# Cross-attention on one core: the value products of two head quads in one run of TensorE, in every second slot

## The chip, the cores and the metric

The kernel runs on one core of one Trainium2 chip. The metric is the time on the device in microseconds (us); a kernel is run several times, and the median counts. Everything is in float32. TensorE (PE) multiplies, VectorE (DVE), ScalarE (ACT) and GpSimd (POOL) work on tiles in SBUF and PSUM, and all DMAs but two small ones are issued by SyncE (SP), whose queue is worked off in order.

## The reference

A layer of cross-attention over 8 batches of 256 rows and 256 memory slots, with 1024 columns in 32 heads of 32. It is cut here to what is computed:

```python
mu = jnp.mean(hidden_states, axis=-1, keepdims=True)
var = jnp.var(hidden_states, axis=-1, keepdims=True)
x = (hidden_states - mu) * jax.lax.rsqrt(var + LN_EPS) * ln_gamma + ln_beta
Q = _split_heads(x @ Wq.T)
K = _split_heads(memory_keys)
V = _split_heads(memory_values)
scores = jnp.einsum('bhsd,bhtd->bhst', Q, K) * scale
scores = jnp.where(mask, scores, -jnp.inf)
probs = jax.nn.softmax(scores, axis=-1)
attn = jnp.einsum('bhst,bhtd->bhsd', probs, V)
attn = attn.transpose(0, 2, 1, 3).reshape(B, S, HIDDEN)
return residual + attn @ Wout.T
```

Keys and values are both the input `ctx_4096`. The mask is all ones, but the kernel works for any.

## The kernel before, in words

The unit of work is a *quad*: four heads of one batch, which fill the 128 partitions. There are 8 quads in a batch and N = 64 in all. The main loop (L903) has one *slot* per quad n; `b, i = divmod(n - 8, 8)` gives the batch whose output is projected meanwhile, and the place i of the slot in that batch. A kernel is written here in the order in which each engine is to do its work (a manual schedule), and waits follow from the data.

In slot n TensorE is given, in this order:

- `scores(n + 1)` (L471): 8 matmuls on four tiles of 32 rows, into four PSUM banks;
- the output steps of place 0 (`project_steps(n, 0)`);
- `values(n - 2)` (L614), the *value run*: 32 matmuls, probabilities times values, on eight tiles of 64 rows by 32 columns. A float32 matmul is two records of PE and two weight loads, so the run has 64 and 64. It fills two PSUM tiles, and ACT copies them with `copy_at` (L629) into `at`, the operand of the output projection;
- the output steps of place 1, then the query projection (`make_q` L331 in the first slots, later `query_product` L432), then the output steps of place 2.

The output projection of a batch is done by seven products of half-size blocks (a Strassen scheme, `PRODUCTS` L647), each in four steps of 128 rows, so 28 steps a batch. `STEPS` (L654) deals them to nine slots, i = 0 to 8, and in each slot to the three places. Step 0 to 3 are A11, 4 to 7 A12, 8 to 11 S2, then S3, A22, S1 and S4. Step c of A12 reads quad 4 + c of the batch. Blocks and sums are taken or stored between steps by DVE (`take`, `store`), since all go through one PSUM bank. The sums S1 to S4 are made by POOL (`sum_at`). Batch 6 is dealt by `ENDS` to slots 56 to 63, and the last batch is projected in part in slots 59 to 62 and in part behind the loop (L1013 to L1078).

The softmax of quad n + 1 (`softmax_parts`, L491) runs beside slot n on the other engines: DVE takes scores out of PSUM with the mask and the row minimum, ACT takes the exponential, POOL divides, and DVE transposes blocks of 32 into `pT`. A quarter of `pT` stands on wrong partitions; ACT copies it aside into `pc` (`aside`), and four DMAs of SP, the *swaps*, put it in its place (`tail`, L595). Loads named in `ahead` go out before the swaps, those in `between` stand between the first two swaps and the last two. In slots below 8 and above 56 the tail is put off into the next softmax (L604). `copy_at` stands in that stream of ACT behind the first exponentials, or, in slots with i = 1, behind the last.

`load_v` (L140) brings the values of a pair of quads, 512 KB, in odd slots for the next pair, into one of two buffers (`vp`). `pT` has three buffers, `pc` (`asp`) three.

## Time and profile before

| what | us |
|---|---|
| median of 3 runs | 575.77 |
| lowest, highest run | 574.71, 577.12 |
| profiled execution, span | 577.6 |
| PE busy | 567.7 |
| DVE busy | 458.6 |
| ACT busy | 412.1 |
| POOL busy | 404.7 |
| value products on PE (L622), 4096 records | 74.3 |

The profile gives no other time for its execution than the span, from the first instruction to the last. It is 1.8 us above the median and 0.5 above the highest of the runs. PE's granted clock is 0.997 on average.

A line of the timeline has the start, the length, the engine, the line of the kernel, the operation, what is written and read, the shape and the number of records, and in brackets the idle time of the engine before it with what ended it. A line of the waits has who waited for whom, the total in us, the number of times and the longest. A line of the stretches has the stretch, its length, then the busy time of PE, PE's weight loads, DVE, ACT and POOL with the instructions of each, then the granted clock, the share of the DMA engines and GB/s.

### The profile page before, as it was taken

What the parts mean: (1) busy time and instruction counts of PE and PEld (TensorE: products, weight loads), DVE (VectorE), ACT (ScalarE), POOL (GpSimd) and SP (SyncE); (2) the same over time, 40 slices, a digit from 0 to 9 for tenths busy, and PEclk for the clock granted to TensorE, in tenths of its full rate; (3) what the DMA queues carried; (4) which work ended last, traced back from release to release, by engine and by line L of the source; (5) the groups of instructions that cost most, each with busy time, mean ns of one, the idle gap of its engine ahead of it and who ended that gap; (6) DMA issues with size and microseconds to landing.
All of it is one profiled execution on the core that took longest, in us unless ns stands there. A gap on an engine that the chain in (4) does not pass through costs nothing.

```text
span 577.6 us, 20001 instructions
## 1 busy us (share of the span) xinstructions
PE 567.7 (98%) x7162; PEld 392.2 (68%) x7162; DVE 458.6 (79%) x1695; ACT 412.1 (71%) x1425; POOL 404.7 (70%) x672
## 2 busy tenths in 40 slices
PE   8999998999999999899999999999999999999998
PEld 8788884666667777477776677667766777755444
DVE  6897887687878878678888888888877868879823
ACT  4688886677758857678577976779767866869820
POOL 1788998699896896665657775676656667448780
PEclk9999999999999999999999999999999999999999
DMA  8675778756778667776686767887658865436741
GB/s 312 224 211 184 218 240 209 244 172 196 196 229 271 215 188 219 225 222 202 181 247 181 233 196 201 237 257 217 186 160 254 239 192 147 130 112 182 214 154 74
DMA packets 47475, 117.98 MB, mean 204 GB/s; under 512 B 9104, under 2 KB 9872, under 8 KB 47376
## 3 DMA queue, kind: packets, MB, share of 16 engines
q1 hardware_dynamic: 47088, 116.69, 68.2%
q8 instruction: 57, 0.93, 0.7%
q14 instruction: 42, 0.34, 0.2%
q10 hardware_dynamic: 288, 0.01, 0.0%
HBM read 65.28 MB, written 11.53 MB: 133 GB/s over the span
## 4 chain that ended last, share of the span: by engine, by line
PE 79%; POOL 8%; DVE 6%; issue 2%; DMA 2%; ACT 1%; SPq 0%; DVEq 0%; POOLq 0%; ACTq 0%
PE po_S L694 17%; PE pq_A L440 16%; PE sc L479 10%; PE po_A L694 10%; PE pv L622 9%; PE pq_S L440 6%; POOL e L528 6%; PE pq L340 6%; DVE e L515 3%; PE po_end L761 2%; DVE pT L534 1%; PE po_last L761 1%; POOL wo L183 1%; DMA pT<-pT 1%; ACT e L519 1%
## 5 line engine op out<-in xcount | busy, mean ns | idle before, releaser
L528 POOL TENSOR_SCALAR e<-e,rden 128x256 f32<-128x256 f32 x512 | 237.0, 483 | 131.1 <-DVE rden L526 129.6
L519 ACT ACTIVATE e<-e,mn 128x256 f32<-128x256 f32 x512 | 254.0, 500 | 53.8 <-DVE mn L515 53.8
L534 DVE STREAM_TRANSPOSE pT<-e 128x512 f32<-128x512 f32 x256 | 180.7, 707 | 54.8 <-POOL e L528 43.8
L515 DVE CUSTOM_DVE_ANT_0 e<-sc,mb 128x256 f32<-128x256 f32 x512 | 185.9, 416 | 23.7 <-PE sc L479 23.2
L540 ACT COPY pc<-pT 128x512 f32<-128x512 f32 x128 | 79.0, 617 | 72.0 <-DVE pT L534 43.0
L519 ACT ACTIVATION_READ_ACCUMULATOR e<-e,mn 128x1 f32 x512 | 97.7, 191 | 0.0
L340 PE MATMUL pq<-xnT,wq 128*128 128x256 f32 (+1 forms) x368 | 84.1, 383 | 0.0
L340 PEld LDWEIGHTS pq<-xnT,wq 128*128 128x128 f32 x368 | 68.7, 190 | 14.3 <-issue 3.9
L479 PEld LDWEIGHTS sc<-k,qa 32*128 32x128 f32 x1024 | 46.2, 184 | 42.4 <-issue 20.6
L694 PE MATMUL po_S<-wo,at 128*128 128x512 f32 x152 | 74.5, 607 | 0.3 <-DVE r L736 0.3
L622 PE MATMUL pv<-pT,v 64*32 64x128 f32 x4096 | 74.3, 274 | 0.0
L622 PEld LDWEIGHTS pv<-pT,v 64*32 64x32 f32 x4096 | 56.9, 105 | 25.3 <-issue 11.9
L479 PE MATMUL sc<-k,qa 32*128 32x256 f32 x1024 | 73.6, 400 | 0.1
L694 PE MATMUL po_A<-wo,at 128*128 128x512 f32 x128 | 61.9, 616 | 4.2 <-issue 2.2
L694 PE MATMUL po_S<-wo,s 128*128 128x512 f32 x104 | 50.2, 606 | 0.3 <-DVE r L736 0.3
L515 DVE DVE_READ_ACCUMULATOR2_ANT mn<- 128x1 f32 x512 | 42.6, 83 | 0.0
L694 PEld LDWEIGHTS po_A<-wo,at 128*128 128x128 f32 x128 | 22.6, 190 | 29.2 <-issue 23.4
L526 DVE RECIPROCAL rden<-den 128x2 f32<-128x2 f32 x256 | 37.5, 146 | 5.9 <-ACT e L519 4.6
L440 PEld LDWEIGHTS pq_A<-xnT,wq 128*128 128x128 f32 x320 | 37.3, 192 | 4.8 <-issue 4.1
L694 PEld LDWEIGHTS po_S<-wo,at 128*128 128x128 f32 x152 | 25.6, 190 | 20.8 <-issue 19.3
L440 PE MATMUL pq_A<-xnT,wq 128*128 128x128 f32 x320 | 37.3, 275 | 0.0
L635 ACT COPY at<-pv 128x128 f32<-128x128 f32 x128 | 26.2, 253 | 8.7 <-PE pv L622 8.7
(95 smaller groups left out, 605.3 us busy)
## 6 DMA issues: line engine op xcount, KB each, us to landing
v<-in_kv_dram SPq DMA_DIRECT2D x32, 512.0 KB, 4.2
pT<-pT SPq DMA_DIRECT2D x128, 128.0 KB, 2.9
pT<-pc SPq DMA_DIRECT2D x128, 128.0 KB, 4.7
ring<-kept_T SPq DMA_DIRECT2D x18, 512.0 KB, 5.8
k<-in_kv_dram SPq DMA_DIRECT2D x32, 256.0 KB, 3.0
x<-in_x_dram SPq DMA_DIRECT2D x14, 512.0 KB, 5.5
r<-in_x_dram SPq DMA_DIRECT2D x28, 256.0 KB, 4.5
out_dram<-r SPq DMA_DIRECT2D x28, 256.0 KB, 3.9
```

The source lines that it names most:

```text
L340: nc.tensor.matmul(pqs[n], wq[:, o, c, :], xnTs[b](c), start=(c == 0), stop=(c == NC - 1),)
L440: nc.tensor.matmul(pqs[b][:, o, :], w[:, c], x_[:, c], start=begins and o + c == 0, stop=c == NK - 1, skip_group_check=True,)
L479: nc.tensor.matmul(scs[n][j][:, s, :], qa[r, n % NQ, ts(s, P)], ks[n - n % 2][r, n % 2, :], start=True, stop=True,)
L515: nc.vector.tensor_tensor_reduce(out=e[:, s, :], in0=pss[j][:, s, :], in1=mbs[n // NQ], scale=1.0, scalar=NO_SCORE, op0=ALU.add, op1=ALU.m ...
L519: nc.scalar.activation(e[:, s, :], e[:, s, :], AF.Exp, bias=mn[:, s : s + 1], scale=-1.0, accum_out=den[:, s : s + 1],)
L526: nc.vector.reciprocal(rden, dens[j])
L528: nc.gpsimd.tensor_scalar(es[j][:, s, :], es[j][:, s, :], rden[:, s : s + 1], 1.0, ALU.mult, ALU.mult,)
L534: nc.vector.transpose(pT[:, :, :, j, :, :].rearrange("p a i s k -> p (a i) s k"), es[j].rearrange("p s (b t) -> p b s t", t=K),)
L540: nc.scalar.copy(pc[:, :, ts(j, 2)], pT[:, 1, :, ts(j, 2)])
L622: nc.tensor.matmul(pvs[n][r][j * HD : (j + 1) * HD], vs[n - n % 2][ts(r, 2 * K), i, ds(n % 2 * P + j * HD, HD)], pT[ts(r, 2 * K), :, i, j, ...
L635: nc.scalar.copy(ats[b, k][:, c, :, ts(r, 2), :], pv.rearrange("p a s k -> p s a k"))
L694: nc.tensor.matmul(po, operand(b, name)[:, c], wo[:, which, c], start=begins and c == 0, stop=c == NK - 1, skip_group_check=not begins,)
```

## The change

`values` takes one or two quads. Odd slots from 3 on call it with quads n - 3 and n - 2, whose 64 matmuls then stand in one run; even slots have no value products. The two PSUM tiles hold both quads, and `copy_at` moves both in each of its two instructions. Quads 62 and 63 behind the loop stay single.

A quad of an even number is so used one slot later. `pT` gets a fourth buffer; to make room the values have one buffer and `pc` two. `load_v(n - 1)` goes out in odd slot n, ahead of the swaps of that slot's softmax, into the buffer that the value run of the slot has just read. The values of the last pair go into a spare half of an `x` tile, in slot 58.

The 28 output steps are dealt anew over the same nine slots: even slots get more and odd ones fewer. In batch 6 the sum S2 is split two and two instead of three and one, as quad 6 of the batch is now there a slot later.

```diff
-    vp = ctx.enter_context(tc.tile_pool(name="vp", bufs=2))
+    vp = ctx.enter_context(tc.tile_pool(name="vp", bufs=1))
...
-    ptp = ctx.enter_context(tc.tile_pool(name="ptp", bufs=3))
-    asp = ctx.enter_context(tc.tile_pool(name="asp", bufs=3))
+    ptp = ctx.enter_context(tc.tile_pool(name="ptp", bufs=4))
+    asp = ctx.enter_context(tc.tile_pool(name="asp", bufs=2))
...
-        vs[n] = vp.tile([P, NI, 2 * P], F32, tag="v", name=f"v_{n}")
+        if n == N - 2:
+            spare = xp.tile([P, NS, D], F32, tag="x", name=f"v_{n}")
+            vs[n] = spare[:, 0].rearrange("p (i v) -> p i v", i=NI)
+        else:
+            vs[n] = vp.tile([P, NI, 2 * P], F32, tag="v", name=f"v_{n}")
...
-    def values(n):
-        pvs[n] = [
-            ps_v.tile([P, 2, NS, K], F32, tag="pv", name=f"pv_{n}_{r}") for r in range(2)
+    def values(*quads):
+        pair = pvs[quads] = [
+            ps_v.tile([P, len(quads), 2, NS, K], F32, tag="pv", name=f"pv_{quads[0]}_{r}")
+            for r in range(2)
         ]
...
+        for at, n in enumerate(quads):
+            pT = pTs.pop(n)
+            for i in range(NI):
+                for j in range(NH):
+                    for r in range(2):
+                        nc.tensor.matmul(
+                            pair[r][j * HD : (j + 1) * HD, at],
+                            vs[n - n % 2][ts(r, 2 * K), i, ds(n % 2 * P + j * HD, HD)],
+                            pT[ts(r, 2 * K), :, i, j, :, :],
+                            start=(i == 0), stop=(i == NI - 1),
+                        )
...
-        for r, pv in enumerate(pvs.pop(n)):
+        for r, pv in enumerate(pvs.pop(quads)):
             nc.scalar.copy(
-                ats[b, k][:, c, :, ts(r, 2), :], pv.rearrange("p a s k -> p s a k")
-            )
+                ats[b, k][:, ds(c, len(quads)), :, ts(r, 2), :],
+                pv.rearrange("p c a s k -> p c s a k"),
+            )
...
-    STEPS = ((0, 0, 0), (4, 0, 3), (0, 1, 2), (0, 2, 2), (0, 2, 1), (0, 1, 2), (0, 0, 3), (0, 1, 2),
-             (0, 2, 0))
+    STEPS = ((0, 0, 0), (4, 0, 3), (0, 1, 3), (0, 1, 1), (0, 3, 1), (0, 2, 0), (0, 1, 3), (0, 1, 1),
+             (0, 3, 0))
...
-        if n % 2 and n + 1 < N:
-            between.append(partial(load_v, n + 1))
-        elif n % 2 == 0 and n + 4 < N:
+        if n % 2 == 0 and n + 4 < N:
             between.append(partial(load_k, n + 4))
-        ahead = rings[n]
+        ahead = list(rings[n])
...
+        if n % 2 and 3 <= n < N - 1:
+            ahead.insert(0, partial(load_v, n - 1))
+        elif n == N - NQ + 2:
+            ahead.append(partial(load_v, N - 2))
...
-        if n >= 2:
-            values(n - 2)
+        if n >= 3 and n % 2:
+            values(n - 3, n - 2)
...
-            copy_at(n - 2)
+            copy_at((n - 3, n - 2))
...
-            sum_at(b, "S2", *((slice(NK - 1, NK),) if b == B - 2 else ()))
+            sum_at(b, "S2", *((slice(2, NK),) if b == B - 2 else ()))
...
-                sum_at(b, "S2", slice(0, NK - 1))
+                sum_at(b, "S2", slice(0, 2))
```

More of the change, by code (lines that the diff above doesn't have):

```diff
@@ L612, in softmax_parts, with copy_at @@
         yield
-    def values(n):
-        pvs[n] = [
-            ps_v.tile([P, 2, NS, K], F32, tag="pv", name=f"pv_{n}_{r}") for r in range(2)
-        ]
-        pT = pTs.pop(n)
-        for i in range(NI):
-            for j in range(NH):
-                for r in range(2):
-                    nc.tensor.matmul(
-                        pvs[n][r][j * HD : (j + 1) * HD],
-                        vs[n - n % 2][ts(r, 2 * K), i, ds(n % 2 * P + j * HD, HD)],
-                        pT[ts(r, 2 * K), :, i, j, :, :],
-                        start=(i == 0), stop=(i == NI - 1),
-                    )
-    def copy_at(n):
-        b, c = divmod(n, NQ)
+    def values(*quads):
+        pair = pvs[quads] = [
+            ps_v.tile([P, len(quads), 2, NS, K], F32, tag="pv", name=f"pv_{quads[0]}_{r}")
+            for r in range(2)
+        ]
+        for at, n in enumerate(quads):
[9 more added lines that the diff above has]
+                        )
+    def copy_at(quads):
+        b, c = divmod(quads[0], NQ)
         k, c = divmod(c, NK)
@@ L1042, in xattn_kernel @@
     values(N - 2)
-    copy_at(N - 2)
+    copy_at((N - 2,))
     end_sum(slice(2, 3), nc.gpsimd)
@@ L1050, in xattn_kernel @@
     values(N - 1)
-    copy_at(N - 1)
+    copy_at((N - 1,))
     end_sum(slice(3, 4), nc.vector)
```

## The prediction

> **What bounds the kernel.** I read the page's busy shares first, then who TensorE waits for, then its timeline slot by slot, then granted clock by stretch, last the end of the chain.

> ```profile
> PE 567.7 (98%) x7162; PEld 392.2 (68%) x7162; DVE 458.6 (79%) x1695; ACT 412.1 (71%) x1425; POOL 404.7 (70%) x672
> ...
> q8 instruction: 57, 0.93, 0.7%
> ```

> PE is busy 98%; the next, DVE, 79%. What shortens PE's stream shortens the kernel, wherever nothing else is due just behind. The second line is the queue that fetches instructions: 57 packets.

> ```profile
> PE po_A L694 <- issue: 2.2, 1, 2.2
> PE po_A L694 <- DMA wo<-in_woT_dram: 1.7, 1, 1.7
> ...
> PE po_S L694 <- DVE r L736: 0.6, 2, 0.3
> PE po_end L761 <- ACT at L635: 0.4, 1, 0.4
> ```

> These are nearly all of PE's waits. Two early ones are gates: PE waits for `wo` until 98.06, and at 106.15 for DVE's store, whose residual tile landed at 105.22.

> ```profile
> 251.60 1.15 PE L479 MATMUL sc<-k,qa 32*128 32x256 f32 x16
> 252.68 1.16 PE L622 MATMUL pv<-pT,v 64*32 64x128 f32 x64
> 253.76 1.98 PE L694 MATMUL po_S<-wo,s 128*128 128x512 f32 x4
> ```

> One slot's beginning: scores, value products, output steps. From the start of the value run to the start of the next, 1.08 to 1.09 us. Instruction by instruction the run is eight rounds on eight tiles; rounds begin at 0, 133, 242, 351, 461, 570, 679 and 788 ns, and the next run at 1.086 us. A round in the middle takes 0.109 us.

> ```profile
> 240.41 1.16 PE L622 MATMUL pv<-pT,v 64*32 64x128 f32 x64
> 243.75 1.87 PE L694 MATMUL po_A<-wo,at 128*128 128x512 f32 x2 [2.19 <-issue]
> ...
> 244.00:246.00 2.00, 2.00 (x5) 0.97 (x5) 0.34 (x1) 0.65 (x4) 0.00 (x0) 0.50 0.88 258
> ```

> Right behind a value run PE stands for 2.19 us with nothing to wait for. In the trace an instruction packet begins at 241.28, takes 1.10 us, and PE goes on at 243.75: it had run out of instructions. The last line (timeline above, stretches below) has granted clock 0.50: after this idle the trace's clock record stays at half for 3.41 us, so the event cost 2.19 + 1.70 = 3.9 us. A 1.71 us idle before 98.06 left the clock at 1.00.

> ```profile
> 547.67 1.02 PE L761 MATMUL po_last<-wo,at 128*128 128x512 f32 x2
> 548.63 1.16 PE L622 MATMUL pv<-pT,v 64*32 64x128 f32 x64
> 549.71 1.98 PE L761 MATMUL po_end<-wo,at 128*128 128x512 f32 x4
> 552.05 1.98 PE L761 MATMUL po_end<-wo,at 128*128 128x512 f32 x4 [0.36 <-ACT at L635]
> 553.97 1.16 PE L622 MATMUL pv<-pT,v 64*32 64x128 f32 x64
> ```

> The last slot: values of quad 61, two output steps with chunk 0 (quad 60, copied long before) while ACT works through the last softmax, then chunk 1, 0.36 us after ACT's copy.

> **The change, part by part.**

> *Merged value runs.* 64 runs become 31 double and 2 single ones. A second quad in the same run should add eight rounds: 8 x 0.109 = 0.875 us against 1.086 in a run of its own, so 1.961 for two. No double run is in the trace. Bounds for the second quad: 0.788 (from the first round's beginning to the last's) and 1.086 (it saves nothing). I take 0.875, what the rounds show inside one run. The re-entry into full-array matmuls (1.91 us for four records behind a value run against 1.72 behind a query product) is paid in even slots too, behind scores; it is not saved.

> *Where it counts.* What is saved before 106 is lost at the two gates: the load of `wo` was issued at 85.89 behind 1.3 MB, whose sum is not altered by the new order, and the residual at 100.48 behind the same swaps. From 106.15 to the scores of quad 63 (541.98) PE did quads 9 to 59, 51 x 1.086 = 55.39; now pairs (8,9) to (58,59), 26 x 1.961 = 50.99. With 0.29 for the second wait for DVE (149.76; slot 15 now reaches it 0.85 later) the gain is 4.69 us. The new deal of 28 steps changes no count: a step is 0.86 us wherever it stands.

> *The end.* In slot 63 quads 60 and 61 are now one run, and ACT copies both only behind the last softmax. That chain hangs on the scores of 63 and reaches the copies 9.6 us after them (541.98 to 551.57), as before. PE has then done its double run by 549.5 (old clock) and has no chunk 0 to do: it stands until the copies end. Two copies of 256 columns: 253 ns at 128 columns and 617 at 512 give 0.37 each, so about 552.3 against 552.00. Then four steps, 1.91 + 1.72 = 3.63, and values of 62 at 555.93 instead of 553.97: a loss of 1.96. Its bounds: 1.7 (two steps moved behind the copies) and 3.0 (the load of v 60 now goes out behind the two 512 KB loads that landed at 544.26 and 546.90). And the stand of 2.8 us is longer than the 2.19 that cost the clock: 1.70 more, bounds 0 and 1.7; by the nearest row, 1.70. [...]

> *Instructions in time.* PE's 14,554 recorded instructions are 256 to a packet of 16,384 bytes. Anchored at the stall, every packet begins at most 298 instructions ahead of its need, and 0.9 to 6.2 us after PE passes that point (median 1.5; 1.0 to 1.4 where nothing is queued). From packet to resumed PE took 2.47. So PE must need at least 3.5 us for 297 instructions, and more where the queues are full. A value run holds 128 instructions in 1.09 us. Laying the instruction lists of both kernels in such windows, with the trace's durations: before, the shortest is 5.8 us, and it is the very one that stalled; the next is 7.4. After, a double run holds 256 in 1.96 us: behind slot 10 there are three windows of 4.4 to 4.5 (slots 27, 36/37, 39), five of 5.7 to 6.9 and six of 7.1 to 8. Twelve packets of odd slots that were called for as early in the slot came 0.9 to 4.0 late, on the mean 0.29 above the 2.0 that a 4.5 window leaves: 3 x 0.29 = 0.87. In slots with i = 1, with delays 5.8, 5.1, 3.7 and 1.6, the windows of 6.2 and 6.9 cost 0.9 and 0.5 on the mean. Sum 2.3 us, and one half-clock stretch, 1.7. Bounds: 0, and 11 (three stalls of 2.0 + 1.7). [...]

> *One buffer of values.* The load waits for the double run of its slot; behind it on SP's queue stand the swaps of the next quad and the residual loads. SP gets there only after the swaps of the softmax before, 6 to 9 us into the slot; the run ends 3.0 into it (6.7 where i = 1). The load, 4.2 us to landing, has until the next odd slot, 17 us: nothing; with that cover gone PE would wait out what is left of the 4.2. That swaps now queue behind 512 KB (2.2 us) falls on even quads, which are used a slot later.

> *Copies, buffers, steps.* ACT's copy waits for the double run (0.35 us later), with exponentials queued behind; scores find their banks read 3 to 5 us earlier in most slots. At i = 1 the third A12 step now needs quad 6 from this slot: copies done at 7.45, step due at 8.58 (slot from 302.65). With `pc` on two buffers, aside waits for the swap of two slots before, landed 7 us earlier. Each nothing; if the 1.1 us at i = 1 went, 6 slots would pay.

> **Sum.** 577.6 - 3.9 (the profile's own stall) - 4.69 + 1.96 + 1.70 + 2.3 + 1.7 = 576.7. The profiled execution lies 1.8 above the median 575.77 and 0.5 above the highest run; without its stall it would be 573.7, a microsecond under the lowest (574.71). The runs thus hold events of this kind too, and I add none for them. Forecast 576.5.

> **Rivals.**
> - *Fetches keep up, the clock holds:* 573.7 - 4.69 + 1.96 = 571.0, with the clock lost at the end 572.7. For it: 53 of 57 packets came within 5.2 us; against it: the only short window before is the one that stalled.
> - *Slower, by the fetch alone:* double runs outrun the packets. It decides where a packet begins over 2.0 us after its call in a 4.5 window, and each time then loses the clock; two such with 2.0 + 1.7 on top of 572.7 give 580.1, three 583.8. For it: 19 of 51 packets from 60 us on were over 2.0.
> - *The second quad saves nothing:* 26 x 2.172 instead of 50.99 loses the gain and 0.8: with the other terms 582.2; against it: the rounds' even pace. That the runs are not merged is excluded: the built list has 256 value instructions together.

> **How the numbers follow.** My own sum 0.44 (573 to 578.6), the first rival 0.23, the second 0.25, the third 0.08. Half a per cent, about what a measurement of this kernel can tell from no change, is 572.9 to 578.65. The first rival is faster, the second and third slower, mine the same. Eight in ten: 571.8 to 581.5.

> **What would show it.** Value runs of 1.96 us in odd slots only; even slots 8.3 us long; PE "issue" waits right behind double runs, with clock 0.50 after them; some 2.8 us of PE idle before the first po_end, ended by ACT's copy. Wrong it is if double runs take 2.1 or if "issue" stays at nothing.

## The result and the profile after

The changed kernel takes 599.05 us (median of 4 runs, 592.69 to 600.71), and the kernel before took 575.24 beside it: a ratio of 1.0393, 95% interval 1.0335 to 1.0450. The prediction was 576.5 with a range up to 581.5; it was 22.6 us too low, and the change makes the kernel slower.

The profiled execution of the changed kernel has a span of 596.4 us, 18.8 more than the profiled one before (the medians are 23.8 apart; the execution profiled before was a long one, with a stand that the prediction puts at 3.9 us). From its page, the busy times, the queue that fetches instructions, and the chain of work that ended last:

```profile
PE 571.1 (96%) x7162; PEld 398.9 (67%) x7162; DVE 458.1 (77%) x1695; ACT 410.3 (69%) x1363; POOL 403.7 (68%) x672
...
q8 instruction: 56, 0.92, 0.7%
...
PE 65%; DMA 8%; POOL 8%; DVE 8%; ACT 4%; issue 3%; SPq 3%; DVEq 0%; ACTq 0%; POOLq 0%
```

The same chain of the kernel before:

```profile
PE 79%; POOL 8%; DVE 6%; issue 2%; DMA 2%; ACT 1%; SPq 0%; DVEq 0%; POOLq 0%; ACTq 0%
```

DMA has gone from 2% to 8% of the chain, and SP's queue, which was not on it, has 3%. Whom PE waits for in the changed kernel (total, times, longest):

```profile
PE pq_S L444 <- DMA ring<-kept_T: 5.0, 4, 2.8
PE po_A L693 <- ACT qa L353: 4.3, 1, 4.3
PE pv L628 <- DMA pT<-pT: 3.7, 3, 1.5
PE po_end L760 <- ACT at L641: 1.8, 1, 1.8
PE pv L628 <- ACT e L523: 1.4, 1, 1.4
...
PE pv L628 <- issue: 0.5, 1, 0.5
```

Before, the list was led by one stand for instructions and one for `wo`. Now PE waits for the ring's weights, for query copies and for swaps, and hardly for instructions. The start of each slot (its first scores) against the same slot before tells where the 18.8 us come from:

| place | us against before |
|---|---|
| up to slot 9 | -1.0 |
| slot 9 | +5.5 |
| slots 10 to 30, without the kernel before's own stand in slot 26 | +2.5 |
| that stand and its half clock | -3.9 |
| slots 31 to 41 | +6.2 |
| slot 42 (a ring wait of 2.84 us, then half clock) | +5.9 |
| slots 43 to 61 | +1.8 |
| behind the scores of quad 63 | +1.8 |

An odd slot's beginning in the timeline of the changed kernel (start, length, engine, line, operation, shape, records):

```profile
255.82 1.15 PE L483 MATMUL sc<-k,qa 32*128 32x256 f32 x16
256.90 2.11 PE L628 MATMUL pv<-pT,v 64*32 64x128 f32 x128
258.93 1.13 PE L693 MATMUL po_S<-wo,s 128*128 128x512 f32 x2
```

A double run takes 2.03 us from its start to the next operation's (2.036 is usual), where two single ones took 2.17. So the runs are merged and mostly save 0.136 a pair, not 0.211. Three of the 31 do take 1.96 us, the prediction's figure, and 10 of 30 in the fastest kernel below; what sets the two apart is not shown.

Slot 9, PE first, then ACT, then the granted clock (0.50, ahead of the DMA share) in a stretch behind the wait:

```profile
87.13 1.15 PE L483 MATMUL sc<-k,qa 32*128 32x256 f32 x16
92.53 6.34 PE L693 MATMUL po_A<-wo,at 128*128 128x512 f32 x8 [4.26 <-ACT qa L353]
98.81 2.11 PE L628 MATMUL pv<-pT,v 64*32 64x128 f32 x128
```

```profile
91.48 0.62 ACT L544 COPY pc<-pT 128x512 f32<-128x512 f32 x1 [4.58 <-DMA pT<-pc]
92.01 0.83 ACT L353 ACTIVATE qa<-pq,qa 128x256 f32<-128x256 f32 x2
```

```profile
92.40:95.00 2.60, 2.47 (x3) 1.17 (x4) 1.51 (x10) 2.60 (x10) 2.60 (x3) 0.50 0.98 294
```

ACT wants to copy into one of two `pc` buffers that a swap of two quads before still reads; the query copy stands behind it, and PE's next steps need the bank that this copy empties. That swap was issued at 83.14, right behind a load of `wo`, and landed 7.9 us later. Eight records then take 6.34 us at half clock instead of 3.70.

SP's queue in the same stretch of work, the kernel before first:

```profile
226.71 1.14 SPq L600 DMA_DIRECT2D pT<-pT  x2
227.91 0.58 SPq L144 DMA_DIRECT2D v<-in_kv_dram  x1
228.53 0.44 SPq L407 DMA_DIRECT2D ring<-kept_T  x1
229.07 1.15 SPq L604 DMA_DIRECT2D pT<-pc  x2
```

The changed kernel:

```profile
236.22 0.40 SPq L148 DMA_DIRECT2D v<-in_kv_dram  x1
236.72 1.15 SPq L604 DMA_DIRECT2D pT<-pT  x2
237.92 0.57 SPq L411 DMA_DIRECT2D ring<-kept_T  x1
241.41 1.20 SPq L608 DMA_DIRECT2D pT<-pc  x2
```

The last two swaps write where the first two read, so SP holds them until the first two have landed. Before, SP filled that time with the load and stood 0.1 us. Now it stands from 238.49 to 241.41, 2.9 us in which it issues nothing else; the first two swaps land late, behind 512 KB (median to landing 4.2 us against 2.9). It is so throughout: at the 25 even quads from 8 to 56, whose swaps are the ones behind the load, SP stands 1.3 to 6.7 us for their landing, median 3.1 (before, 0.0). This ring load is 9.4 us later than before, though PE is only some 5 us behind. What that ends in, slot 42:

```profile
389.70 1.12 PE L693 MATMUL po_A<-wo,at 128*128 128x512 f32 x2
390.66 1.95 PE L444 MATMUL pq_S<-sx,ring 128*128 128x128 f32 x16
395.45 3.78 PE L444 MATMUL pq_S<-sx,ring 128*128 128x128 f32 x16 [2.84 <-DMA ring<-kept_T]
```

And the end:

```profile
563.55 1.02 PE L760 MATMUL po_last<-wo,at 128*128 128x512 f32 x2
565.16 2.22 PE L628 MATMUL pv<-pT,v 64*32 64x128 f32 x128 [0.59 <-DMA v<-in_kv_dram]
569.18 3.70 PE L760 MATMUL po_end<-wo,at 128*128 128x512 f32 x8 [1.80 <-ACT at L641]
572.81 1.16 PE L628 MATMUL pv<-pT,v 64*32 64x128 f32 x64
```

All four steps stand behind ACT's copy, as the prediction had it.

### The profile page after: what moved, and what is told of

The parts are those of the page before. It is cut to its first block, busy times and chain, and to the rows that moved or that the text cites. A ratio compares the mean times of both kernels' runs of the same rounds, so it can differ in the third digit from the quotient of the medians.

```text
span 596.4 us, 19956 instructions
## 1 busy us (share of the span) xinstructions
PE 571.1 (96%) x7162; PEld 398.9 (67%) x7162; DVE 458.1 (77%) x1695; ACT 410.3 (69%) x1363; POOL 403.7 (68%) x672
## 4 chain that ended last, share of the span: by engine, by line
PE 65%; DMA 8%; POOL 8%; DVE 8%; ACT 4%; issue 3%; SPq 3%; DVEq 0%; ACTq 0%; POOLq 0%
PE po_S L693 15%; PE pq_A L444 10%; PE pq L344 9%; PE pv L628 8%; PE sc L483 8%; POOL e L532 6%; PE po_A L693 5%; PE pq_S L444 4%; DVE e L519 3%; DMA pT<-pT 3%; PE po_end L760 3%; ACT e L523 2%; DVE pT L538 2%; DMA r<-in_x_dram 2%; DMA ring<-kept_T 2%
## 5 line engine op out<-in xcount | busy, mean ns | idle before, releaser
L628 PE MATMUL pv<-pT,v 64*32 64x128 f32 x4096 | 68.2, 272 | 6.6 <-DMA pT<-pT 3.7
L628 PEld LDWEIGHTS pv<-pT,v 64*32 64x32 f32 x4096 | 59.3, 105 | 22.0 <-issue 19.0
L693 PE MATMUL po_A<-wo,at 128*128 128x512 f32 x128 | 63.5, 632 | 4.9 <-ACT qa L353 4.3
L693 PE MATMUL po_S<-wo,s 128*128 128x512 f32 x104 | 52.0, 624 | 0.7 <-issue 0.5
L530 DVE RECIPROCAL rden<-den 128x2 f32<-128x2 f32 x256 | 37.8, 148 | 15.2 <-ACT e L523 14.2
L519 DVE DVE_READ_ACCUMULATOR2_ANT mn<- 128x1 f32 x512 | 42.6, 83 | 0.0
L641 ACT COPY at<-pv 128x256 f32<-128x256 f32 (+1 forms) x66 | 20.6, 363 | 19.3 <-PE pv L628 18.9
## 6 DMA issues: line engine op xcount, KB each, us to landing
k<-in_kv_dram SPq DMA_DIRECT2D x32, 256.0 KB, 3.1
r<-in_x_dram SPq DMA_DIRECT2D x28, 256.0 KB, 5.1
out_dram<-r SPq DMA_DIRECT2D x28, 256.0 KB, 2.7
```

The costliest lines, as they stand in the source:

```text
L519: nc.vector.tensor_tensor_reduce(out=e[:, s, :], in0=pss[j][:, s, :], in1=mbs[n // NQ], scale=1.0, scalar=NO_SCORE, op0=ALU.add, op1=ALU.m ...
L530: nc.vector.reciprocal(rden, dens[j])
L628: nc.tensor.matmul(pair[r][j * HD : (j + 1) * HD, at], vs[n - n % 2][ts(r, 2 * K), i, ds(n % 2 * P + j * HD, HD)], pT[ts(r, 2 * K), :, i, ...
L641: nc.scalar.copy(ats[b, k][:, ds(c, len(quads)), :, ts(r, 2), :], pv.rearrange("p c a s k -> p c s a k"),)
L693: nc.tensor.matmul(po, operand(b, name)[:, c], wo[:, which, c], start=begins and c == 0, stop=c == NK - 1, skip_group_check=not begins,)
```

## The experiments

Three theories. Q: the load's place ahead of the swaps blocks SP's queue. P: two buffers of `pc` make ACT wait. M: the merged runs (late instructions among it) or the new deal of steps. The kernel before ran beside each group, with a median of 575.1 to 575.5.

**One part at a time.** The changed kernel with the load between the swaps:

```diff
-            ahead.insert(0, partial(load_v, n - 1))
+            between.insert(0, partial(load_v, n - 1))
```

> The changed kernel, but the load of values stands between the first two swaps and the last two, as before the change; one buffer of values, two of pc, double runs and deal stay. Theory Q (the load ahead of the swaps blocks SP's queue): swaps land in about 2.9 us again instead of 4.2, ACT's 14.2 us of waits for the pc swaps and PE's waits for swaps and for the ring mostly go, and 577 to 583 us are left: 575.2, less 26 x 0.136 for the double runs (2.036 measured against 2 x 1.086), plus 2 to 4 at the end, plus 2 to 7 for what stays. Theory P (pc on two buffers is what delays ACT and so the query copies): 590 to 598, with ACT's waits for pc still over 8 us. Theory M (the merged runs themselves or the new deal of steps): 594 to 600.

The kernel before with its load ahead of the swaps:

```diff
-        if n % 2 and n + 1 < N:
-            between.append(partial(load_v, n + 1))
...
+        if n % 2 and n + 1 < N:
+            ahead = [partial(load_v, n + 1)] + ahead
```

> The kernel before, with one thing moved: in odd slots the load of values goes out ahead of the swaps; two buffers of values and all else as before. Theory Q: swaps land in over 4 us, PE waits for swaps, ring and query copies, and the time is 585 to 600, at least 10 us over the kernel before. Theories P and M: 574 to 578, as nothing that they name is touched.

The kernel before with `pc` on two buffers:

```diff
-    asp = ctx.enter_context(tc.tile_pool(name="asp", bufs=3))
+    asp = ctx.enter_context(tc.tile_pool(name="asp", bufs=2))
```

> The kernel before, with pc on two buffers instead of three and nothing else. Theory P: ACT waits for the pc swaps for some 10 us in all, and the time is 580 to 590. Theory Q: the swaps land early enough here, since nothing stands ahead of them: 574.5 to 577, ACT's waits for pc under 3 us.

The kernel before with the new deal of steps:

```diff
-    STEPS = ((0, 0, 0), (4, 0, 3), (0, 1, 2), (0, 2, 2), (0, 2, 1), (0, 1, 2), (0, 0, 3), (0, 1, 2),
-             (0, 2, 0))
+    STEPS = ((0, 0, 0), (4, 0, 3), (0, 1, 3), (0, 1, 1), (0, 3, 1), (0, 2, 0), (0, 1, 3), (0, 1, 1),
+             (0, 3, 0))
```

> The kernel before, with the changed kernel's deal of the 28 output steps of batches 0 to 5 and nothing else. Theory M, as far as it rests on the deal: 579 or more, by waits of output steps for sums or copies. Theories Q and P, and the step's price of 0.86 us wherever it stands: 574 to 577.

Measured: 591.49 (ratio 1.0258, 1.0202 to 1.0315), 595.94 (1.0370, 1.0330 to 1.0410), 575.58 (1.0018, 0.9994 to 1.0042) and 575.90 (1.0006, 0.9984 to 1.0027). The load's place alone costs the kernel before 20.5 us; the deal costs nothing, and two `pc` buffers cost nothing there. SP in the second kernel:

```profile
309.65 0.41 SPq L144 DMA_DIRECT2D v<-in_kv_dram  x1
310.14 1.15 SPq L600 DMA_DIRECT2D pT<-pT  x2
311.34 0.57 SPq L407 DMA_DIRECT2D ring<-kept_T  x1
315.37 1.14 SPq L604 DMA_DIRECT2D pT<-pc  x2
```

SP stands 3.5 us, and four waits of PE for the ring, 8.3 us in all, follow. SP's whole time in waits for the first two swaps to land goes with the load's place, in this kernel and in others below:

| kernel | SP waits for `pT<-pT`, us | times | longest |
|---|---|---|---|
| before | 42.6 | 34 | 5.1 |
| changed | 142.0 | 58 | 6.7 |
| before, load ahead | 146.6 | 61 | 6.0 |
| before, load ahead by ACT's queue | 80.5 | 53 | 4.7 |
| changed, load between in slots 7 to 55 | 48.6 | 46 | 4.3 |

Theory Q holds, but the first kernel gave back only 7.6 of 23.8 us, less than it expected. It has new waits of its own:

```profile
PE pv L628 <- DMA v<-in_kv_dram: 5.9, 3, 3.2
PE pv L628 <- issue: 5.6, 2, 3.2
PE po_S L693 <- issue: 3.0, 1, 3.0
```

In slots below 7 and above 55 the swaps are put off to the next slot, and a load between them with them: it then comes too late for the values (slots 5, 59 and 61 are 14.5, 11.5 and 11.2 us long, in the changed kernel 8.5, 7.6 and 7.6). The two waits of the second line fall in slot 59 and behind the scores of quad 63, with no packet of instructions near, so they are probably of the same kind. The third line is slot 37, to which I come back.

**In whose queue, and the rest of the change.** The changed kernel with the load between the swaps only where they go out at once:

```diff
-            ahead.insert(0, partial(load_v, n - 1))
+            (between if NQ - 2 < n < N - NQ else ahead).insert(0, partial(load_v, n - 1))
```

> The changed kernel, with the load of values between the swaps in slots 7 to 55, where the swaps go out at once, and ahead of them, as in the changed kernel, in the other odd slots, where they are put off to the next slot (there the load between the swaps came too late in the run before this one: 5.9 us of PE's waits for values, in slots 5, 59 and 61). All else of the change stays. Theory Q: 575.4, less 26 x 0.136 = 3.5, plus 2.0 to 3.7 at the end, plus 0 to 3 for a fetch: 574 to 578, no PE wait for swaps, ring or query copies over 1 us in all. If something else in the change costs as much as the load's place: 585 or more.

With the end undone (the values of quads 60 and 61 in the second half of the spare `x` tile, loaded in slot 58, those of 62 and 63 in slot 60):

```diff
+        if n >= N - 2:
+            values(n - 2)
-        if n >= 3 and n % 2:
+        elif n >= 3 and n % 2:
             values(n - 3, n - 2)
...
-            copy_at((n - 3, n - 2))
+            copy_at((n - 2,))
```

> The kernel just described, with quads 60 and 61 in runs of their own again, in slots 62 and 63, and their values in the other half of the spare x tile. Theory of the end (two more steps stand behind ACT's copies): 1.5 to 3.7 us less than the kernel just described, po_end waits of 0.4 us for ACT's copy instead of 1.8, and with theory Q 571 to 575, at or below the kernel before. If the end costs nothing: the same as the kernel just described.

With 24 pairs taken apart again inside their slot (`apart`: odd slots 9 to 55; `values` takes the part of the pair that it is to do):

```diff
+        if apart and i == 1:
+            values(n - 3, n - 2, part=slice(0, 1))
         project_steps(n, 0)
...
+            elif i > 1:
+                values(n - 3, n - 2, part=slice(0, 1))
         project_steps(n, 1)
+        if apart:
+            values(n - 3, n - 2, part=slice(1, 2))
```

> The kernel just described, with the two quads of 24 pairs (slots 9 to 55) in two runs of the same slot, with the output steps of the slot's middle between them; tiles, copies and loads stay as they are. A double run takes 2.036 us and two single ones 2.172: if the merge saves that and no more, 24 x 0.136 = 3.3 us longer; if it saves what the prediction had (0.211), 5.1; if runs of double length lose to late instructions what they save, the same time or less.

The kernel before with the load ahead, but by the other queue:

```diff
-        nc.sync.dma_start(
+        (nc.scalar if n else nc.sync).dma_start(
             vs[n], kv[b, g // 2, :, 2 * T :]
```

> The kernel before with the load of values issued at the same place as in the second run of the first job, ahead of the swaps, but by ACT's queue instead of SP's. If what counts is the order within SP's queue (swaps that stand behind 512 KB in it, and SP waiting for them): 575 to 580. If what counts is that 512 KB move over the same 16 DMA engines just then, in whatever queue: 588 to 596, as with SP's queue.

Measured: 581.54 (1.0138, 1.0086 to 1.0190), 579.85 (1.0080, 1.0055 to 1.0106), 597.22 (1.0380, 1.0345 to 1.0415) and 578.08 (1.0039, 1.0012 to 1.0066). The last one says what about the load's place counts: the same bytes at the same point of the program cost 2.6 us from ACT's queue and 20.5 from SP's, and the swaps land in time again:

```profile
pT<-pT SPq DMA_DIRECT2D x128, 128.0 KB, 2.9
...
v<-in_kv_dram ACTq DMA_DIRECT2D x31, 512.0 KB, 5.0
```

With the load in SP's queue the first line had 4.7. In both kernels the load is gone from the gap between the swaps, and here SP stands 1.2 us (median) at the same even quads, with the load in its own queue 3.1. So the gap alone accounts for 2.6 us at most, and the rest comes of swaps that land late behind the load. One thing more differs, though: ACT issues its load 2.7 us ahead of the next swap (median of the loads for quads 10 to 54), SP 0.6. So the order within a queue is not parted from this head start, and 512 KB that start just ahead of the swaps from another queue are untested; which of the two brings the 4.7 us down to 2.9 is not shown.

The first two kernels are 6.0 and 4.3 us above the kernel before, 3.5 and 4.9 above the top of what Q alone expected: slot 9 still waits 4.6 and 4.4 us for the query copy, so theory P has its place there. In the kernel before with two buffers the same wait was 2.8 us, but it took the place of the wait for `wo` (slot 9 was 11.4 us long against 11.0). Two buffers are not the only way to it: the kernel before with the load ahead in SP's queue has three, and PE waits 4.1 us for the same query copy (slot 9 is 15.0 us long). There DVE's statistics stand 3.98 us for an `x` tile, with the transposes and the copy aside behind them. The end gave 1.7. The third kernel, expected 3.3 to 5.1 slower, was 17.4 slower and prices nothing: the early run in slots with i = 1 comes before its load has landed (PE waited 4.0 us for values and 5.8 once without a named releaser), and the slots with i = 3 and 5 are 0.4 longer, not 0.136, probably by a second entry into full-array products (in the kernel before 1.91 us for four records behind a value run, 1.72 behind a query product).

**Slot 9, and all three undone.** The query copies of slot 8 go ahead of the copy aside:

```diff
-        if n <= NQ:
+        if n <= NQ + 1:
             for copy in copies:
                 copy()
```

In the changed kernel:

> The changed kernel with one thing moved: in the softmax of quad 9 (slot 8) ACT's two query copies stand ahead of its first copy aside, not behind it. In the changed kernel TensorE waits there 4.26 us for a query copy, which stands behind a copy aside that waits for the swap of two quads before (pc on two buffers), and then runs at half clock. If that is the cause of slot 9's 5.5 us: slot 9 shorter by 3 to 5.5 us (the load of wo is the next gate there), ACT still waiting for the swap, the rest of the kernel as before, 593 to 596 in place of 599.05. If slot 9 waits for something else: no change, 597 to 600.

On top of the load between the swaps and the end undone:

> The same move on top of the kernel with the load of values between the swaps in slots 7 to 55 and with the end undone (579.85 median, in which slot 9 still loses some 4 us against the kernel before). If the three causes named (the load's place, pc's two buffers in slot 9, the end) are all: 574 to 577, of which the merged runs hold a gain of about 0.9 us a batch and late instructions in slots 27 and 37 a loss of 0 to 5; below 573 only if instructions come in time. If something is still missing: 578 or more.

Measured: 598.12 (1.0401, 1.0351 to 1.0450) and 579.34 (1.0058, 1.0026 to 1.0090). In the changed kernel slot 9 went from 16.5 to 11.8 us, as expected, and yet the whole gained 0.9, within its spread: by slot 35 the lead over the changed kernel was down from 4.1 to 0.2 us, in waits for values, ring and swaps. Where PE waited for what SP issues, an earlier PE waited longer. The second kernel shows why the merge still did not pay. It keeps the kernel before's pace or better in all slots but a few; the worst is slot 37:

```profile
332.07 2.01 PE L629 MATMUL pv<-pT,v 64*32 64x128 f32 x127
338.37 0.27 PE L629 MATMUL pv<-pT,v 64*32 64x128 f32 x1 [4.28 <-issue]
```

A packet of instructions begins at 335.86, takes 1.13 us, and PE goes on at 338.37, 2.51 later (2.47 in the kernel before's stand). It is one of the slots that the prediction's layout had named (27, 36/37, 39), and the stands of 3.00 and 2.01 us in the kernels above were there too, one of 2.73 in slot 27.

**Where the packets end.** Fewer or more of the transposes at the start move all later instructions against their packets of 256 (from the first packet's start to the last's, PE began 254.8 instructions a packet in the kernel before and 256.0 in the changed one):

```diff
-    for _ in range(32):
+    for _ in range(20):
         nc.tensor.transpose(busy, ident, ident)
```

> The kernel of the last run (load between the swaps, end undone, copies ahead of the copy aside; 579.34 median), with 20 instead of 32 of the transposes that keep TensorE busy while the first x tile is loaded. It moves TensorE's later instructions by 24 places in their packets of 256, and nothing else. In the last run TensorE stood 4.28 us in slot 37 beside a packet that began at 335.86, and 1.05 in slot 11. Theory F (late instruction packets): laid out with the durations of the trace, the last run has windows of 4.2 to 4.7 us in slots 11, 27, 37 and 39; this one has 3.9 in slot 5 and then none under 5.0 (slot 37), 5.4 (27), 5.6 (39). The stand in slot 37 is shorter than 2 us or gone, no other over 2 us behind slot 9, and the median is 573 to 577. If slot 37 waits for something else, the stand stays there and the median is 578 to 580.

With `range(52)`:

> The same with 52 transposes instead of 32, which moves the instructions by 40 places the other way, and makes the first 7 us some 2.6 us longer, of which the waits of slot 9 take most. Theory F: the windows of slots 27, 37 and 39 are now 5.7 to 6.2 us, and the shortest are 4.8 in slots 7 and 51 and 5.1 in slot 29: stands, where there are any, are in slots 7, 29 and 51, none over 1 us is in slot 37, and the median is 574 to 579. If slot 37 waits for something else, the stand stays there.

Measured: 572.80 (0.9963, 0.9942 to 0.9984), a little faster than the kernel before, and 575.17 (0.9996, 0.9981 to 1.0010). Slot 37 is 8.5 and 8.6 us long instead of 14.7; with 20 transposes:

```profile
332.34 2.03 PE L629 MATMUL pv<-pT,v 64*32 64x128 f32 x128
334.30 1.98 PE L694 MATMUL po_S<-wo,at 128*128 128x512 f32 x4
```

With 20, PE stands 0.85 us in slot 5 (the short window), 0.29 in slot 27 and 1.12 in slot 15, which the layout had not named. With 52, no stand shows where it could have, and 2.91 us are lost in slot 9. Where PE ran out of instructions was set by where the packets end: 6.5 us of the 579.34 with 20, 4.2 with 52.

**One cause at a time put back** into the kernel of 572.80, and the kernel before with the 20 transposes of the diff above:

> The kernel before with 20 instead of 32 transposes at the start, as in the kernel of 572.80. Its shortest window grows from 5.8 us (slot 26, in which its profile showed the stand of 2.19 us) to 7.4. If the merged runs are what put that kernel ahead of the kernel before: 575 to 576, no change, and the merge is worth 2.5 us. If it was the place of the packets: 572 to 573.5, the stand of slot 26 is gone, and the merge is worth nothing that shows. From the slots of even pace (0.8 us a batch, six batches) I expect the former in the larger part: 573.5 to 575, the merge worth 1 to 3.

The load ahead everywhere:

```diff
-            (between if NQ - 2 < n < N - NQ else ahead).insert(0, partial(load_v, n - 1))
+            ahead.insert(0, partial(load_v, n - 1))
```

> The kernel of 572.80 with the load of values ahead of the swaps in all odd slots, as in the change; the other causes stay taken away. Theory Q, the load's place is the largest cause: 583 to 592, with PE's waits for swaps and ring back in slots with i = 1 and 2. If the causes only matter together: under 578.

The end's diff reversed:

> The kernel of 572.80 with the end as in the change (quads 60 and 61 in one run of slot 63). The prediction's two terms for it were 1.96 and 1.70 for the clock; the changed kernel's trace held the clock, with a stand of 1.80 us. So 574.5 to 575.5; 576.5 with the clock lost; 572.8 if other waits cover it.

The copies' diff reversed:

```diff
-        if n <= NQ + 1:
+        if n <= NQ:
```

> The kernel of 572.80 with the query copies of slot 8 behind the copy aside again. Slot 9 waits some 4.4 us for the query copy and loses the clock: 575.5 to 578, as slot 9 was 15.3 us long with it and 11.4 to 12.4 without. If the gate of wo takes it: 573.

| kernel | median us | ratio to the kernel before | against 572.80 |
|---|---|---|---|
| kernel before, 20 transposes | 573.90 | 0.9983 (0.9966 to 1.0000) | +1.1 |
| load ahead of the swaps | 595.87 | 1.0339 (1.0323 to 1.0354) | +23.1 |
| end as in the change | 576.37 | 1.0022 (0.9994 to 1.0051) | +3.6 |
| query copies behind the copy aside | 578.67 | 1.0057 (1.0043 to 1.0070) | +5.9 |

The load's place costs nearly as much alone as the whole change. It came out 3.9 us above its expected range, the end and the copies 0.9 and 0.7 above theirs. PE's waits with it:

```profile
PE pv L629 <- DMA pT<-pT: 5.6, 3, 2.4
PE pq_S L445 <- DMA ring<-kept_T: 4.7, 3, 1.9
PE pv L629 <- issue: 3.1, 3, 1.8
```

With the copies put back, one wait of 4.6 us in slot 9 and the half clock behind it. The end's profile is 5.5 us over, of which 1.9 come behind the scores of quad 63 and 2.7 in slot 27, where PE stands 2.1 us for instructions and then has half the clock. Not every execution has this: the four of ten with a granted clock of 1.000 took 572.3 to 575.1, the others 576.1 to 580.8. So 1.9 is the end's own price, and the 3.6 hold late instructions too. The causes don't add up: 572.80 + 23.1 + 5.9 + 3.6 is 605.4, over the 599.05, since waits for SP cover others.

## Why the prediction was wrong

The step that failed is the one under *One buffer of values*: "That swaps now queue behind 512 KB (2.2 us) falls on even quads, which are used a slot later", costed at nothing. Its delay was right in size (for even quads alone 4.7 us to landing against 2.6, where the profile gives it). But I followed only PE's use of these swaps. Behind them in SP's queue stand two swaps that wait for their landing, and the load had been the work that filled the wait. Put ahead of all four, it makes SP stand some 3 us in nearly every odd slot, and what is late next is everything that SP issues: ring weights, swaps, residuals, values. Measured by itself: 20.5 us in the kernel before, 23.1 in the merged one, where I had 0.

The second failed step is the sentence on `pc` under *Copies, buffers, steps*: "aside waits for the swap of two slots before, landed 7 us earlier. Each nothing". In slot 9 the swap is behind the load of `wo` and lands late; the copy aside waits 4.58 us, query copies and PE behind it. By itself 5.9 us, with the order of ACT's copies put back; a third `pc` buffer in the changed kernel wasn't tried. "If the 1.1 us at i = 1 went, 6 slots would pay" named the right slots, not the right wait: PE waits 1.13 to 1.48 in slots 25, 33 and 41, for swaps ahead of the value run, a late consequence of the first failure.

The other terms:

- *Merged value runs*, 51 runs for 26, 4.69 us: mis-sized. In most runs the second quad costs 0.95 us, not 0.875; 26 x 0.136 is 3.5. At even pace the merged kernels gain 0.6 to 0.75 us a batch of four pairs, where four times 0.136 are 0.54.
- *The end*, 1.96 for the steps: right in mechanism and size (1.8, and 1.7 between two medians). 1.70 for the clock: wrong; the stand was 1.80 us, not 2.8, and the clock held (1.00 from 568 to 572).
- *Instructions in time*, 2.3 + 1.7: the mechanism was right, and two of the three slots (27 and 37), the size not. In the changed kernel it hardly shows (1.4 us of stands), probably because PE waits for SP so often that packets keep up; no run tests that. With those waits gone it is 6.5, more than I had.
- *The deal of steps costs nothing:* right (575.90).

The rivals. That fetches keep up is wrong for the merge, as 6.5 us show. The rival of late fetches priced the slow side at 580.1 to 583.8; the kernel with the load between the swaps and the copies ahead, and without the loss at the end (1.8 to 3.6 more), is at 579.34. So that rival describes about what the merge would have cost had the load and `pc` been free, though by one stand of 4.28 us and not two or three of 2.0, and it is no account of 599.05. No rival of mine had SP's queue in it.

The merge itself is worth about 1 us (572.80 against 573.90, intervals that overlap); with so little, that stays open. Three buffers of `pc` beside four of `pT` weren't tried.

## What to carry to other kernels

Ask of a moved DMA what it did where it was and what will stand behind it where it goes. Between two transfers of which the second waits for the first, an independent load was free here (SP stood 0.0 us, median); ahead of both it made the first land late (4.7 us against 2.6), and the whole queue stood (3.1 us). Then follow the queue, not only the buffer: what is issued behind it, and who needs that within the next slots. And where many small instructions stand together on TensorE, lay them out against the packets that bring them; moving the packet boundary by 24 instructions was worth 6.5 us, the merge about 1.

## What the runs showed of the hardware

Where PE stood for an instruction packet, it went on 2.2 to 2.9 us after the packet began (22 stands of 0.4 us or more in 13 kernels; 2.47 in the kernel before, 2.51 in slot 37 above), though the packet itself took 0.9 to 1.6 (1.10 and 1.13 in these two).
